# Where the last twelve weighted sums of an attention block stand in TensorE's order

## The chip, the cores and the metric

The kernel runs on one core of a Trainium2 chip. The metric is the device time of one execution in microseconds (us), as the median of several runs. A core has five engines that work through their own queues in order: TensorE (PE; its weight loads are listed as PEld), VectorE (DVE), ScalarE (ACT), GpSimd (POOL) and SyncE (SP, which issues DMAs). They wait for each other by semaphores.

## What is computed

A layer of convolutions and a selective scan, then an additive attention, then a normalised recurrence, on a tensor of 4 images with 128 channels and 4096 positions. The change is in the attention, which for each image computes

```python
q = einsum('bld,ud->blu', x, Wt)            # U = 32 units
k = einsum('bld,ud->blu', x, Wx)
beta = tanh(q[:, :, None, :] + k[:, None, :, :] + bh)
alpha = einsum('bsju,u->bsj', beta, Wa[:, 0]) + ba[0]
alpha = softmax(tanh(alpha), axis=-1)
c_r = einsum('bsj,bjd->bsd', alpha, x)      # the weighted sums
t = t + c_r
```

## The kernel before

`_bounded` runs three stages one after the other: `_layer0` (up to about 3900 us), `_rational` (the attention, to about 11430 us) and `_chunked` (the recurrence). Within each the order of the instructions is written out by hand: an engine runs what the code issues to it in the order in which the code issues it.

`_rational` works through 4 images of 8 blocks each; a block is 512 queries (`QB`), and its tiles are the 32 groups (`JT`) of 128 keys. It doesn't compute the 32 hyperbolic tangents of a pair one by one. It groups the 32 units in six groups, of 6, 6, 5, 5, 5 and 5 units. For each group the sum of the tangents is a fraction, whose denominator and numerator are each one matrix product of exponentials of the keys (`F`) with exponentials of the queries (`E`, and `cE`, weighted). The groups stand in pairs: `A` holds the two groups of six units, each a product over 64 rows; `B1` and `B2` hold two groups of five units each, products over 32 rows. `products` (line 1209) issues them, through `lower` for the denominators and `upper` for the numerators.

For a tile and a pair of groups the work is this:
- `lower` (line 1217): two matmuls on TensorE into one denominator buffer `pd` (two banks of PSUM; the pool has two such buffers).
- `inverse` (line 1229): on ScalarE a logarithm (line 1231), which reads `pd` and so frees it, and an exponential (line 1232). The result is `ra` for `A`, `rb` for `B1` and `B2`.
- `upper` (line 1222): two matmuls into two numerator buffers `pn` (one bank each; the pool has three).
- `times` (line 1225): on VectorE, two multiplications of `ra` or `rb` by the two `pn` (line 1227); each frees one `pn`.
- GpSimd adds the three pairs (lines 1346 and 1333), and VectorE adds the two halves of the sum into `A[:, jt, :]` (line 1343).

Every matmul here is recorded as two instructions (passes). The loop over the tiles is at lines 1323 to 1350. For tile `jt` TensorE gets, in this order: the denominators `dA`; the numerators `nB2` of the tile before; the denominators `dB1`; the numerators `nA`; the denominators `dB2`; the numerators `nB1`. At the end of a tile the list `between` may add work: functions registered for a tile number, called in line 1349.

After the last tile of a block, `A` is turned into weights in four parts (`PARTS`, line 1380) by a tanh and an exponential on ScalarE. The weighted sum of a tile is one matmul over all 128 rows into the buffer `ct` (`weighted`, line 1356, recorded as line 1357), accumulated over the 32 tiles. The sums of tiles 0 to 19 (`NOW` = 20) are issued there. Those of tiles 20 to 31 are left: `between[2 + i]` receives one each, for tiles 2 to 13 of the next block. The division and the output of the old block follow as further entries of `between` in tiles 14 to 22 (`CLOSE_AT`), and the normalisation of the next image, its queries and its transposes also stand in `between`, at tiles 15 to 29. The very last block issues all its sums at once. So 31 of the 32 blocks have twelve such sums in their tiles, 372 in all.

Of the kernel before, what the change touches and what calls it, by code (L numbers as in the profile page):

```python
# [1045 lines left out]
def _rational(ctx, tc, k, x1, x2, top, Wt, Wx, bh, Wa, ba):  # L1046
# [20 lines left out]
    def ln_exp():  # L1067
        nc.scalar.preload_act_table_set("natural_log_exp_and_others")
# [7 lines left out]
    def pw():  # L1076
        return psW.tile([P, QB], F32, name="ct", tag="ct")
# [62 lines left out]
    def norm_load(b, xn, cols):  # L1140
        nc.sync.dma_start(xn[:, cols], x1[b, :, cols])

    def norm_steps(xn, cols, alloc):

        xc = xn[:, cols]
        n = cols.stop - cols.start
        held = {}

        def centre():
            ps = alloc()  # L1150
            _mm(nc, ps, k.avg, xc, n)
            nc.vector.tensor_tensor(xc, xc, ps, ALU.subtract)

        def square():
            held["sq"] = rb.tile([P, CH], F32, name="sq", tag="rb")[:, 0:n]
            nc.scalar.activation(held["sq"], xc, AF.Square)

        def rate():
            ps = alloc()
            _mm(nc, ps, k.avg, held["sq"], n)  # L1160
            _rsqrt(nc, held["sq"], ps, k.eps5)

        def scale():
            nc.gpsimd.tensor_tensor(xc, xc, held["sq"], ALU.mult)

        return centre, square, rate, scale

    def keys(F, xn, c, ps, i):

        exponent(ps, w_k, xn[:, blocks[c]], i, F[:, i, blocks[c]], b_k[:, i : i + 1])  # L1170
# [23 lines left out]
    def queries(E, xn, s, i):  # L1194
        exponent(pw(), w_q, xn[:, s * QB : (s + 1) * QB], i, E[:, i, :])
# [21 lines left out]
    def lower(unit, F, jt, E):  # L1217
        ps = pd()
        products((ps[:, 0, :], ps[:, 1, :]), unit, F, jt, E)
        return ps  # L1220

    def upper(unit, F, jt, cE):
        return products((pn(), pn()), unit, F, jt, cE)

    def times(r, ns):
        for a in range(2):
            nc.vector.tensor_tensor(r[:, a, :], r[:, a, :], ns[a], ALU.mult)  # L1227

    def inverse(d, pool, tag):
        r = pool.tile([P, 2, QB], F32, name=tag, tag=tag)  # L1230
        nc.scalar.activation(r, d, AF.Ln, scale=LOWER)  # L1231
        nc.scalar.activation(r, r, AF.Exp, scale=-1.0)  # L1232
        return r
# [58 lines left out]
    start = 0  # L1292
    first = lower("A", F, 0, E), lower("B1", F, 0, E)
    between = {}
    for c in range(1, nq):
        for i in range(2):
            between.setdefault(2 * c - 2 + i, []).append(lambda c=c, i=i, xn=xn: keys(F, xn, c, pw(), i))
    for c in range(nq):
        between.setdefault(16 + c, []).append(lambda c=c, xn=xn: turn(xT, xn, c))
    for b in range(B):  # L1300
        upcoming = None
        for s in range(nq):
            more = s + 1 < nq or b + 1 < B
            turned = s + 1 == nq and b + 1 < B
            xr = sb.tile([P, QB], F32, name="xr")
            nc.sync.dma_start(xr, x1[b, :, blocks[s]])
            if b + 1 < B:

                if s == 0:
                    upcoming = two.tile([P, L], F32, name="xn")  # L1310
                norm_load(b + 1, upcoming, blocks[s])
                for at, go in zip(NORM_AT, norm_steps(upcoming, blocks[s], pn)):
                    between.setdefault(at, []).append(go)
            if more:
                E_next = two.tile([P, 2, QB], F32, name="E")
                of = upcoming if turned else xn
                for i in range(2):
                    between.setdefault(QUERIES_AT[i], []).append(
                        lambda i=i, s=s, of=of, E_next=E_next: queries(E_next, of, (s + 1) % nq, i)
                    )  # L1320
            ln_exp()
            late = None
            for jt in range(start, JT + 1):
                if jt < JT:
                    dA = lower("A", F, jt, E) if jt > start else first[0]
                if late is not None:
                    pj, rA_, rB2_ = late
                    nB2 = upper("B2", F, pj, cE)
                if jt < JT:
                    dB1 = lower("B1", F, jt, E) if jt > start else first[1]  # L1330
                if late is not None:
                    times(rB2_, nB2)
                    nc.gpsimd.tensor_tensor(rA_, rA_, rB2_, ALU.add)  # L1333
                if jt < JT:
                    nA = upper("A", F, jt, cE)
                    rA = inverse(dA, ra, "ra")
                    times(rA, nA)
                    dB2 = lower("B2", F, jt, E)
                    nB1 = upper("B1", F, jt, cE)
                    rB1 = inverse(dB1, rb, "rb")  # L1340
                    times(rB1, nB1)
                if late is not None:
                    nc.vector.tensor_tensor(A[:, pj, :], rA_[:, 0, :], rA_[:, 1, :], ALU.add)  # L1343
                if jt == JT:
                    break
                nc.gpsimd.tensor_tensor(rA, rA, rB1, ALU.add)  # L1346
                rB2 = inverse(dB2, rb, "rb")
                late = jt, rA, rB2
                for go in between.pop(jt, ()):
                    go()  # L1350

            if more:
                E, cE = E_next, weigh(E_next)
            ct = pw()

            def weighted(jt, ct=ct, xT=xT):
                nc.tensor.matmul(ct, xT[:, jt, :], A[:, jt, :], start=(jt == 0), stop=(jt == JT - 1))  # L1357

            held = {}

            def ahead(step):
                if not more:
                    return
                if step == 0:
                    held["A"], held["B1"] = lower("A", F, 0, E), lower("B1", F, 0, E)
                    held["A"] = direct(held["A"], upper("A", F, 0, cE), ra, "ra")
                elif step == 1:
                    held["B2"] = lower("B2", F, 0, E)  # L1370
                    held["B1"] = direct(held["B1"], upper("B1", F, 0, cE), rb, "rb")
                    nc.gpsimd.tensor_tensor(held["A"], held["A"], held["B1"], ALU.add)
                elif step == 2:
                    held["first"] = lower("A", F, 1, E)
                    r = direct(held["B2"], upper("B2", F, 0, cE), rb, "rb")
                    nc.gpsimd.tensor_tensor(held["A"], held["A"], r, ALU.add)
                else:
                    held["first"] = held["first"], lower("B1", F, 1, E)

            for i, (lo, hi) in enumerate(PARTS if more else LAST_PARTS):  # L1380
                nc.scalar.activation(A[:, lo:hi, :], A[:, lo:hi, :], AF.Tanh, bias=b_a)  # L1381
                nc.scalar.activation(A[:, lo:hi, :], A[:, lo:hi, :], AF.Exp)  # L1382
                if i == 0:
                    if turned:

                        F = big.tile([P, 2, L], F32, name="F")
                        for c in range(nq):
                            all_keys(F, upcoming, c)
                    ahead(0)
                if hi <= NOW or not more:  # L1390
                    for jt in range(lo, hi):
                        weighted(jt)
                if more and i + 1 < len(PARTS):
                    ahead(i + 1)
            if more:
                nc.vector.tensor_tensor(A[:, 0, :], held["A"][:, 0, :], held["A"][:, 1, :], ALU.add)
                first = held["first"]
                start = 1
            between = {}

            todo = closing(b, s, ct, xr, 4 if more else 1)
            if more:
                for i, jt in enumerate(range(NOW, JT)):
                    between[2 + i] = [lambda jt=jt, weighted=weighted: weighted(jt)]
                for at, go in zip(CLOSE_AT, todo):
                    between[at] = [go]
            else:
                for go in todo:
                    go()
            if turned:  # L1410
                xn = upcoming
                xT = big.tile([P, JT, P], F32, name="xT")
                for c in range(nq):
                    between.setdefault(22 + c, []).append(lambda xT=xT, xn=xn, c=c: turn(xT, xn, c))
# [247 lines left out]
```

## Time and profile before

| what | value |
|---|---|
| median of 3 runs | 11655.28 us (11652.04 to 11657.58) |
| the profiled execution, its own time | 11654.41 us |
| its span in the profile | 11652.7 us |
| TensorE, VectorE, ScalarE, GpSimd busy, 5000 to 6000 us | 964.60, 744.27, 958.39, 702.72 us |
| L1212, numerators, 12288 instructions | 4728.8 us busy, 650 ns each |
| L1212, denominators, 12288 instructions | 3478.0 us busy, 648 ns each |
| L1231 and L1232 for `rb`, 1986 each | 1011 and 1057 ns each |
| L1227 for `rb`, 3972 instructions | 682 ns each |
| L1346 and L1333 on GpSimd, 993 each | 2653 and 2363 ns each |
| L1357, the weighted sums, 2048 instructions | 641 ns each |

The times of the profile are from one execution, counted from the start of its span. "Busy" is the time in which an engine had an instruction in work; records of TensorE overlap, since products over few rows run side by side in the array, and several are merged into one line of a timeline ("x4"). In a timeline a line has the start, the duration, the engine, the line of code, the operation, what is written and what is read, and in brackets how long the engine stood idle before and what released it. In the list of waits a line has who waited, for whom, the total in us, how many times and the longest.

### The profile page before, as it was taken

To read this page: it belongs to the slowest core of one execution; us is meant where nothing else is said; L and a number is where in the kernel's file an instruction comes from. 1 tells how busy PE (TensorE), PEld (TensorE's weight loads), DVE (VectorE), ACT (ScalarE), POOL (GpSimd) and SP (SyncE) were. 2 spreads that over 40 slices of the span, in tenths; PEclk is the share of its full clock that TensorE was granted. 3 is DMA by queue.
4 is the path that set the end of the run, shared out by engine and by line. 5 is a ranking of instruction groups with operands and counts; after the bars stand their busy time and mean duration, and the time that the engine had idled before them with its cause. 6 is when DMAs were issued, how large, how long until landed. Compare 5 with 4: busy or idle time off the path is not lost.

```text
span 11652.7 us, 111820 instructions
## 1 busy us (share of the span) xinstructions
PE 10307.6 (88%) x36210; PEld 3184.3 (27%) x36210; DVE 8997.6 (77%) x10066; ACT 9520.9 (82%) x10209; POOL 8625.1 (74%) x3703
## 2 busy tenths in 40 slices
PE   6787787778777699999999999999999999999997
PEld 2121121122111133333333333333333333333334
DVE  4998899889889677777777777777777777777773
ACT  3566556656655599999999999999999999999996
POOL 3999889889889677767766776767677767776773
PEclk8898898889888799999999999999999999999998
DMA  4888778778778300000000000000000000000001
GB/s 118 189 182 194 171 177 193 170 182 190 179 171 186 79 1 3 6 3 3 6 3 3 3 6 3 3 3 6 3 3 3 6 2 3 3 4 3 2 3 60
DMA packets 225332, 737.77 MB, mean 63 GB/s; under 512 B 41104, under 2 KB 41936, under 8 KB 223712
## 3 DMA queue, kind: packets, MB, share of 16 engines
q1 hardware_dynamic: 221760, 729.96, 26.5%
q8 instruction: 286, 4.69, 0.2%
q14 instruction: 310, 2.54, 0.1%
q10 hardware_dynamic: 2976, 0.58, 0.0%
HBM read 612.95 MB, written 117.44 MB: 63 GB/s over the span
## 4 chain that ended last, share of the span: by engine, by line
PE 50%; ACT 9%; DVE 4%; issue 3%; POOL 0%; DMA 0%; DVEq 0%; POOLq 0%; SPq 0%; ACTq 0%
PE pn L1212 26%; PE pd L1212 16%; PE ct L1357 4%; ACT A L1381 3%; ACT A L1382 2%; DVE rb L1227 2%; ACT rb L1231 1%; ACT rb L1232 1%; PE ct L1134 1%; ACT ra L1231 1%; DVE rb L1239 1%; PE vy L1556 0%; DVE A L1343 0%; PE pn L56 0%; PE ct L1262 0%
## 5 line engine op out<-in xcount | busy, mean ns | idle before, releaser
L1212 PE MATMUL pn<-cE,F 32*128 32x512 f32 (+1 forms) x12288 | 4728.8, 650 | 196.6 <-DVE rb L1227 88.5
L1227 DVE TENSOR_TENSOR rb<-rb,pn 128x512 f32<-128x512 f32 x3972 | 2544.5, 682 | 1310.9 <-PE pd L1212 684.9
L1212 PE MATMUL pd<-E,F 32*128 32x512 f32 (+1 forms) x12288 | 3478.0, 648 | 20.9 <-DVE ra L1239 15.7
L1346 POOL TENSOR_TENSOR ra<-ra,rb 128x1024 f32<-128x1024 f32 x993 | 2634.5, 2653 | 957.2 <-DVE rb L1227 956.9
L1333 POOL TENSOR_TENSOR ra<-ra,rb 128x1024 f32<-128x1024 f32 x993 | 2346.8, 2363 | 409.0 <-DVE rb L1227 348.4
L626 POOL TENSOR_TENSOR dBu<-dtdu,bbcc 128x1024 f32<-128x1024 f32 x1024 | 2398.3, 2368 | 216.9 <-DMA dtdu<-ddd 155.5
L1232 ACT ACTIVATE rb<-rb 128x1024 f32<-128x1024 f32 x1986 | 2099.6, 1057 | 62.8
L1212 PEld LDWEIGHTS pn<-cE,F 32*128 32x128 f32 (+1 forms) x12288 | 1418.0, 185 | 2574.8 <-DVE rb L1227 1066.6
L1231 ACT ACTIVATE rb<-pd 128x1024 f32<-128x1024 f32 x1986 | 2007.6, 1011 | 89.9 <-PE pn L1212 75.2
L668 PE MATMUL py<-h,gather 128*32 128x512 f32 x4096 | 1297.9, 699 | 477.3 <-POOL h L651 364.5
L1227 DVE TENSOR_TENSOR ra<-ra,pn 128x512 f32<-128x512 f32 x1986 | 1317.9, 684 | 231.4 <-ACT ra L1232 175.6
L1212 PEld LDWEIGHTS pd<-E,F 32*128 32x128 f32 (+1 forms) x12288 | 931.4, 185 | 1638.5 <-issue 693.7
L621 ACT ACTIVATE pa<-dtdu,a_neg 128x1024 f32<-128x1024 f32 x1024 | 1145.3, 1119 | 53.1 <-DVE h L641 32.1
L651 POOL TENSOR_TENSOR h<-h,bbcc 128x1024 f32<-128x1024 f32 x384 | 912.0, 2375 | 346.2 <-ACT carry L649 338.5
L641 DVE TENSOR_TENSOR_SCAN pa<-pa,carry,dBu 128x1024 f32<-128x1024 f32 x480 | 1124.7, 2343 | 23.1 <-ACT pa L621 11.3
L1232 ACT ACTIVATE ra<-ra 128x1024 f32<-128x1024 f32 x993 | 1049.6, 1057 | 31.4
L1357 PE MATMUL ct<-A,xT 128*128 128x512 f32 x2048 | 1050.9, 641 | 8.2 <-ACT A L1382 8.2
L1231 ACT ACTIVATE ra<-pd 128x1024 f32<-128x1024 f32 x993 | 1008.7, 1016 | 60.0 <-PE pd L1212 26.5
L649 ACT COPY carry<-pa 128x1 f32<-128x1 f32 x640 | 102.4, 160 | 1043.7 <-DVE h L648 1041.9
L1343 DVE TENSOR_TENSOR A<-ra 128x512 f32<-128x512 f32 x993 | 745.0, 750 | 116.3 <-POOL ra L1333 116.0
L648 DVE TENSOR_TENSOR h<-pa,bbcc 128x1024 f32<-128x1024 f32 x640 | 784.1, 1225 | 59.0 <-PE py L668 0.9
L641 DVE TENSOR_TENSOR_SCAN h<-pa,carry,dBu 128x1024 f32<-128x1024 f32 x288 | 675.0, 2344 | 171.1 <-PE py L668 148.2
(291 smaller groups left out, 8731.3 us busy)
## 6 DMA issues: line engine op xcount, KB each, us to landing
bbcc<-bcd SPq DMA_DIRECT2D x1024, 256.0 KB, 6.9
dtdu<-ddd SPq DMA_DIRECT2D x1024, 256.0 KB, 7.1
ddd<-dd SPq DMA_DIRECT2D x64, 1024.0 KB, 5.1
src<-src SPq DMA_DIRECT2D x64, 512.0 KB, 8.3
xs<-in_x_dram SPq DMA_DIRECT2D x16, 512.0 KB, 7.5
src<-xs SPq DMA_DIRECT2D x16, 512.0 KB, 3.0
bcd<-bc SPq DMA_DIRECT2D x64, 128.0 KB, 2.0
src<-xsT SPq DMA_DIRECT2D x16, 512.0 KB, 5.4
```

The source lines that it names most:

```text
L621: nc.scalar.activation(dA, its[m].DT[r][:, 0, :], AF.Exp, scale=a)
L626: nc.gpsimd.tensor_tensor(dBu, its[m].DT[r][:, 1, :], its[m].BC[q][:, 0, :], ALU.mult)
L641: nc.vector.tensor_tensor_scan(to[:, step], dA[:, step], live.pop(("dBu", u))[:, step], 0.0 if m % nch == 0 else its[m - 1].carry[:, col : ...
L651: nc.gpsimd.tensor_tensor(h, h, cc, ALU.mult)
L668: nc.tensor.matmul(it.y[to, c], gather, live["h", v][:, c], start=False, stop=(q == QS - 1))
L1212: nc.tensor.matmul(ps[a], F[lo:hi, i, jt * P : (jt + 1) * P], side[lo:hi, i, :], start=True, stop=True)
L1227: nc.vector.tensor_tensor(r[:, a, :], r[:, a, :], ns[a], ALU.mult)
L1231: nc.scalar.activation(r, d, AF.Ln, scale=LOWER)
L1232: nc.scalar.activation(r, r, AF.Exp, scale=-1.0)
L1333: nc.gpsimd.tensor_tensor(rA_, rA_, rB2_, ALU.add)
L1346: nc.gpsimd.tensor_tensor(rA, rA, rB1, ALU.add)
L1357: nc.tensor.matmul(ct, xT[:, jt, :], A[:, jt, :], start=(jt == 0), stop=(jt == JT - 1))
```

## The change

The twelve sums are registered in a second list, `middle`, which is called at another place of the tile: after `dB1` and after the multiplication and addition of `B2` of the tile before, and ahead of `nA`. The tile numbers stay 2 to 13. All other entries of `between` stay where they are.

```diff
--- before
+++ after
@@ -1292,6 +1292,7 @@
     start = 0
     first = lower("A", F, 0, E), lower("B1", F, 0, E)
     between = {}
+    middle = {}
     for c in range(1, nq):
         for i in range(2):
             between.setdefault(2 * c - 2 + i, []).append(lambda c=c, i=i, xn=xn: keys(F, xn, c, pw(), i))
@@ -1331,6 +1332,8 @@
                 if late is not None:
                     times(rB2_, nB2)
                     nc.gpsimd.tensor_tensor(rA_, rA_, rB2_, ALU.add)
+                for go in middle.pop(jt, ()):
+                    go()
                 if jt < JT:
                     nA = upper("A", F, jt, cE)
                     rA = inverse(dA, ra, "ra")
@@ -1401,7 +1404,7 @@
             todo = closing(b, s, ct, xr, 4 if more else 1)
             if more:
                 for i, jt in enumerate(range(NOW, JT)):
-                    between[2 + i] = [lambda jt=jt, weighted=weighted: weighted(jt)]
+                    middle[2 + i] = [lambda jt=jt, weighted=weighted: weighted(jt)]
                 for at, go in zip(CLOSE_AT, todo):
                     between[at] = [go]
             else:
```

TensorE's order in tiles 2 to 13 was `dA`, `nB2`, `dB1`, `nA`, `dB2`, `nB1`, sum; it becomes `dA`, `nB2`, `dB1`, sum, `nA`, `dB2`, `nB1`.

## The prediction

> **What bounds the kernel now.** I read the page's busy times and its chain first, then the waits inside the attention stretch (4200 to 11200 us), then the timeline of single tiles.
>
> ```profile
> PE 10307.6 (88%) x36210; PEld 3184.3 (27%) x36210; DVE 8997.6 (77%) x10066; ACT 9520.9 (82%) x10209; POOL 8625.1 (74%) x3703
> ...
> PE pn L1212 26%; PE pd L1212 16%; PE ct L1357 4%; ACT A L1381 3%; ACT A L1382 2%; DVE rb L1227 2%; ACT rb L1231 1%; ACT rb L1232 1%; PE ct L1134 1%; ACT ra L1231 1%; DVE rb L1239 1%; PE vy L1556 0%; DVE A L1343 0%; PE pn L56 0%; PE ct L1262 0%
> ```
>
> The chain names TensorE, and in the attention TensorE is busy 0.97 of the time, but ScalarE is at 0.96 beside it (windows of 1000 us), so a busy share decides nothing. The waits say what TensorE lacks:
>
> ```profile
> PEld pn L1212 <- DVE rb L1227: 1013.0, 1381, 2.9
> DVE rb L1227 <- PE pd L1212: 660.8, 688, 2.5
> PEld pn L1212 <- DVE ra L1227: 210.8, 346, 1.5
> ```
>
> The numerators (`pn`) wait for a PSUM bank that VectorE's multiplication L1227 gives back. Now one tile that holds a weighted sum (I call it the sum matmul; L1357, two passes):
>
> ```profile
> 6208.88 1.13 PE L1212 MATMUL pd<-E,F 64*128 64x512 f32 x4
> 6209.94 0.70 PE L1212 MATMUL pn<-cE,F 32*128 32x512 f32 x2
> 6210.06 1.02 ACT L1231 ACTIVATE ra<-pd 128x1024 f32<-128x1024 f32 x1
> 6211.01 2.02 PE L1212 MATMUL pn<-cE,F 64*128 64x512 f32 x4
> 6211.17 1.28 DVE L1227 TENSOR_TENSOR rb<-rb,pn 128x512 f32<-128x512 f32 x2 [1.36 <-PE pd L1212]
> 6211.91 0.29 PEld L1212 LDWEIGHTS pn<-cE,F 64*128 64x128 f32 x2 [0.61 <-DVE rb L1227]
> 6212.37 1.39 DVE L1227 TENSOR_TENSOR ra<-ra,pn 128x512 f32<-128x512 f32 x2
> 6212.97 0.70 PE L1212 MATMUL pd<-E,F 32*128 32x512 f32 x2
> 6214.16 1.12 PE L1357 MATMUL ct<-A,xT 128*128 128x512 f32 x2
> 6214.20 1.02 ACT L1231 ACTIVATE rb<-pd 128x1024 f32<-128x1024 f32 x1
> 6215.21 0.70 PE L1212 MATMUL pd<-E,F 64*128 64x512 f32 x2
> ```
>
> and one that holds none and no other extra work:
>
> ```profile
> 6320.28 0.70 PE L1212 MATMUL pn<-cE,F 32*128 32x512 f32 x2
> 6321.30 1.01 ACT L1231 ACTIVATE ra<-pd 128x1024 f32<-128x1024 f32 x1
> 6323.43 1.29 DVE L1227 TENSOR_TENSOR ra<-ra,pn 128x512 f32<-128x512 f32 x2 [0.63 <-ACT ra L1232]
> 6324.17 0.29 PEld L1212 LDWEIGHTS pn<-cE,F 32*128 32x128 f32 x2 [0.56 <-DVE ra L1227]
> 6325.22 1.13 PE L1212 MATMUL pd<-E,F 64*128 64x512 f32 x4
> 6326.28 0.70 PE L1212 MATMUL pn<-cE,F 32*128 32x512 f32 x2
> ```
>
> The second tile is bound by ScalarE: three Ln/Exp pairs at 2.00 us each, 6.00 us from one start of the logarithm `ra<-pd` to the next. The first is bound by TensorE: 6.33 us (6208.88 to 6215.21). There six-unit numerators `A` (6211.01) take 2.02 us, where the same form for the denominators takes 1.13: their second half stands still until 6211.91 for the bank of `rb`. The timeline gives the same cadence for all 31 blocks that hold such sums: tile 2 takes 6.15, tiles 3 to 13 6.33 each (a handful of stray tiles apart, by about 0.2), tile 14 6.16. Their sum is 6.15 + 11 x 6.33 + 6.16 = 81.94 us; ScalarE alone would need 13 x 6.00 = 78.00.
>
> **What the Trainium skill says.** "Perfetto Trace Analysis", Identifying the Most-Contended Engine, warns that matmul busy time is no measure of nearness to peak; the trace agrees, as the 2.02 us record holds 0.9 us of waiting. The same page, Identifying Performance Opportunities, reads a gap that repeats as a want of buffers; here it is the third `pn` bank. "TensorEngine Tiling (Array Packing)", Key Properties, says that a change of tiling mode drains TensorE. The sum matmul (full array) stands between a 32-row and a 64-row group before and after, so a tile has five changes either way; the trace shows 1.05 us from the sum matmul to the next group (6214.16 to 6215.21), no visible drain. "TensorE: Matmul & The Clock Gate", What's actually happening, puts the array at half rate after idle windows of 3.4 us that run freely; the clock record here has half-rate stretches of 3.4, 6.8 and 10.2 us. I use that below.
>
> **The change, part by part.** Per tile 2 to 13 of 31 blocks, one sum matmul (372 in all) goes from the end of TensorE's tile to the place between `dB1` and `nA`. Nothing is added or removed; no DMA and no instruction of another queue moves, and VectorE's and GpSimd's orders stay. On TensorE it is moved past `nA`, `dB2` and `nB1`. Its data (a slice of `A` of the old block, `xT`) were ready before the block began, so it waits for nothing.
>
> I set zero at the start of the group `nB2`+`dB1` (6209.94) and carry the lags of the two tiles over.
> - The group: 1.07 (6209.94 to 6211.01). The sum matmul: 1.05, so it ends at 2.12.
> - VectorE starts on `rB2` at 1.23 and returns its first bank 0.74 later (6211.17 to 6211.91), at 1.97. So `nA` finds both banks at 2.12: the stall of 0.90 is filled, by a matmul of 1.05.
> - What is late next: `nB1`'s second half needs the bank of `nA`'s first half, that is `times(rA)`. In today's sum tile `nA`'s first half runs ahead alone, and `rA` starts at 2.43, so `nB1` loses only 0.13 (the group from 6212.97 takes 1.19). Now `nA` starts at 2.12, `rA` at 2.12 + 1.23 = 3.35, its bank returns at 4.09 (0.74, also 6323.43 to 6324.17), `nB1` ends 1.05 later (6324.17 to 6325.22) at 5.14, `dA` of the next tile takes 1.06, and the next group starts at 6.20.
>
> The tile without a sum checks this sum: there `rA` starts at 3.15, because the exponential ends then, and 3.15 + 0.74 + 1.05 + 1.06 = 6.00. So the new sum tile takes 6.20 on TensorE against 6.33, and ScalarE's 6.00 is not reached. The move trades 0.90 of stall at `nA` for one of 0.77 more at `nB1`.
>
> Over a block: on entry TensorE is 1.02 us ahead of the logarithm (6320.28 against 6321.30; tile 2 the same) and loses 0.20 per tile. Tiles 2 to 5 therefore keep ScalarE's 6.00 (24.00). Then `dB2`, which ends at 2.12 + 1.05 + 1.23 = 4.40, holds the third logarithm: tile 6 takes 6.18, tiles 7 to 13 6.20 each (43.40), tile 14 6.06 as the lead comes back. Sum 79.64, against 81.94: 2.30 us per block, times 31 = 71 us. Covers: VectorE has 0.84 us to spare before `rA` at 3.35 (free at 2.51), the exponential ends near 2.30, GpSimd needs 2.36 + 2.67 = 5.03 per tile. None is short.
>
> Against this stands the half-rate clock. Once a block, in tile 22, VectorE holds TensorE up for 2.08 us or more, and by its phase against the 3.41 us grid that tile takes 7.78 (no half rate, blocks 10, 12, 14), about 9.3 (one window), or about 10.8 (two). The mean of blocks 1 to 23 is 9.54, 1.76 over 7.78. Blocks 3 to 6 and 18 to 22 sit at a period near 228.8, which is 67 windows (228.7), with one window each. A shorter block leaves this lock: its bare period goes from 227.16 to 224.86, 0.42 under 66 windows, so the phase walks through all cases. Following the phase by the prices above I get mostly two windows in two blocks of three: (2 x 3.05 + 1.55)/3 = 2.5 a block, up 0.7. Over 23 blocks that is 17 us given back; I take 14, since each turn to a new image sets the phase anew. Bounds from both sides: no half rate at all in these tiles gives 1.76 x 23 = 40 us more gain, two windows in each (3.05 - 1.76) x 23 = 30 us less.
>
> Sum against the profiled execution: span 11652.7, execution 11654.41; minus 71, plus 14 gives 11597.4. The median of the runs shown, 11655.28, is 0.9 above, so 11598 us.
>
> **The rivals.**
> - Full gain: `nB1` doesn't stall, and the sum tiles fall to ScalarE's 6.00. 3.94 x 31 = 122 us, 11533. For it: TensorE's work is only 5 x 1.06 = 5.3 us per tile. Against: the wait for `ra` at 6324.17 is there already in the tile without a sum.
> - No gain: `times(rB2)` is made to wait for the sum matmul too, or the half-rate windows take it. With the first, `rB2` starts at 2.28, its bank returns at 3.02, `nA`'s second half ends at 4.08, and 1.19 + 1.06 lead to 6.33: no difference, 11655. For it: today's wait names the `pd` matmul right ahead in the queue. Against: the multiplications are issued ahead of the sum matmul, so they have no reason to wait for it. The clock alone takes at most 30 of 71.
> - Slower: the full-array sum matmul between two groups that feed VectorE drains the array, where it costs nothing visible today, and `nA`'s results, `rA` and the bank for `nB1` all come late. From 0.18 us per tile (period 6.38) it outweighs the gain; at 0.30 the tiles take 6.50, the thirteen 12 x 6.50 - 0.82 (the lead) + 6.06 = 83.2, 1.3 x 31 = 40 us more: 11695. For it: `nA` lies on the chain and today's place has slack behind it. Against: the 1.05 us above, with the same neighbours.
>
> **How the numbers follow.** Partial gain 0.63 (its own range 11560 to 11632), full gain 0.09 (11500 to 11560), no gain 0.15 (11632 to 11678), slower 0.13. The range 11530 to 11675 leaves out the slower case and half of the full gain, under 2 in 10. A change of 0.2%, 23 us, is about what a measurement can tell from none. Faster: 0.63 + 0.09, less 0.02 of the first near its edge, 0.70. Within: 0.16. Slower: 0.14.
>
> **What would show it.** Right: logarithm starts 6.00 apart in tiles 2 to 5 and 6.20 in 7 to 13; the row of `pn` weight loads waiting for `rb` falls by some 0.61 x 372 = 227 us and that for `ra` grows by about 0.56 x 372 = 208 us (the recorded gaps at 6211.91 and 6324.17); `nA` in 1.13 us. Wrong: 6.33 or more in tiles 7 to 13 (no gain, slower), 6.00 in all (full), or tile 22 above 10.5 in every block.

## The result, and the profile after

The changed kernel takes 11598.17 us (median of 5 runs, 11595.65 to 11604.05), the kernel before in runs beside it 11653.49. The ratio is 0.9953, with a 95% interval of 0.9942 to 0.9964: faster by 0.5%, 55 us. The profiled execution took 11599.52 us, its span 11597.8, which is 54.9 less than the span before.

The page of the changed kernel, busy times and chain, looks almost as it did:

```profile
PE 10265.4 (89%) x36210; PEld 3139.3 (27%) x36210; DVE 8992.9 (78%) x10066; ACT 9467.7 (82%) x10209; POOL 8626.5 (74%) x3703
...
PE pn L1212 26%; PE pd L1212 16%; PE ct L1360 4%; ACT A L1384 4%; ACT A L1385 2%; DVE rb L1227 2%; ACT rb L1231 1%; ACT rb L1232 1%; PE ct L1134 1%; ACT ra L1231 1%; PE vy L1559 1%; DVE A L1346 0%; PE ct L1262 0%; PE pn L56 0%; ACT L1384 0%
```

Shares don't tell the two apart; the change is seen in a tile. The added lines shift the line numbers: the sum is now L1360, GpSimd's additions are L1334 and L1349, VectorE's is L1346. This is a tile with a sum in the timeline of the changed kernel:

```profile
6179.27 0.70 PE L1212 MATMUL pn<-cE,F 32*128 32x512 f32 x2
6180.34 1.12 PE L1360 MATMUL ct<-A,xT 128*128 128x512 f32 x2
6180.50 1.28 DVE L1227 TENSOR_TENSOR rb<-rb,pn 128x512 f32<-128x512 f32 x2 [0.89 <-ACT ra L1231]
6181.40 0.30 PEld L1212 LDWEIGHTS pn<-cE,F 64*128 64x128 f32 x4 [0.76 <-DVE rb L1227]
6181.40 1.13 PE L1212 MATMUL pn<-cE,F 64*128 64x512 f32 x4
6182.46 0.70 PE L1212 MATMUL pd<-E,F 32*128 32x512 f32 x2
6182.62 1.29 DVE L1227 TENSOR_TENSOR ra<-ra,pn 128x512 f32<-128x512 f32 x2 [0.84 <-PE pn L1212]
```

The sum runs while VectorE frees `rb`'s bank; `nA` (6181.40) then needs 1.13 us where it took 2.02. One tile earlier in the same timeline the other end is seen: the multiplication `ra` waits for `nA`, and `nB1`'s second half for that.

```profile
6173.06 0.70 PE L1212 MATMUL pn<-cE,F 32*128 32x512 f32 x2
...
6176.42 1.28 DVE L1227 TENSOR_TENSOR ra<-ra,pn 128x512 f32<-128x512 f32 x2 [0.84 <-PE pn L1212]
6176.79 1.49 PE L1212 MATMUL pn<-cE,F 32*128 32x512 f32 x3
6177.16 0.29 PEld L1212 LDWEIGHTS pn<-cE,F 32*128 32x128 f32 x2 [0.61 <-DVE ra L1227]
6178.21 1.13 PE L1212 MATMUL pd<-E,F 64*128 64x512 f32 x4
```

From one group `nB2`+`dB1` to the next it is 6.21 us (6173.06 to 6179.27), against 6.33. The waits between 4200 and 11200 us, one line of the kernel before and then three of the changed one:

```profile
DVE ra L1227 <- PE pn L1212: 24.1, 41, 1.0
```

```profile
PEld pn L1212 <- DVE rb L1227: 1333.6, 1728, 2.9
...
PEld pn L1212 <- DVE ra L1227: 416.6, 686, 1.4
...
DVE ra L1227 <- PE pn L1212: 320.3, 387, 1.2
```

The last was 24.1 us before: VectorE now waits 0.84 us in most sum tiles. The one for `ra` grew by 206. The one for `rb` rose, although the wait it is named for is gone. The timeline shows why: the load at 6181.40 carries "0.76 <-DVE rb", but by the 0.74 us that a bank took to return before, it was free near 6181.24 (6180.50 + 0.74), and the load starts only 1.06 after the sum's start. I read this as the load standing behind the running sum: the name is that of the semaphore that came last, not of what held the engine.

From the starts of the logarithm `ra<-pd` in both traces, the span's 54.9 us divide like this (a tile's time is from its own logarithm to the next tile's):

| stretch | before | after | difference |
|---|---|---|---|
| tiles 2 to 14 of blocks 1 to 31 | 2541.8 (81.99 a block) | 2477.3 (79.91 a block) | -64.4 |
| tile 22 of blocks 1 to 23 | 219.4 (9.54 each) | 231.1 (10.05 each) | +11.7 |
| the other tiles from 15 to 30 | 2956.0 | 2951.4 | -4.6 |
| everything else | | | +2.4 |

Of the -4.6, 3.4 us lie in tiles 24 and 25 of blocks 24 to 31. There is no next image to normalise there, and in six of these blocks TensorE stands still for 1.8 us in tile 24, not in tile 22.

### The profile page after: what moved, and what is told of

It reads as the page before. It is cut to its first block, busy times and chain, and to the rows that moved or that the text cites. A ratio compares the mean times of both kernels' runs of the same rounds, so it can differ in the third digit from the quotient of the medians.

```text
span 11597.8 us, 111820 instructions
## 1 busy us (share of the span) xinstructions
PE 10265.4 (89%) x36210; PEld 3139.3 (27%) x36210; DVE 8992.9 (78%) x10066; ACT 9467.7 (82%) x10209; POOL 8626.5 (74%) x3703
## 3 DMA queue, kind: packets, MB, share of 16 engines
q14 instruction: 311, 2.54, 0.1%
## 4 chain that ended last, share of the span: by engine, by line
PE 50%; ACT 10%; DVE 3%; issue 3%; POOL 0%; DMA 0%; POOLq 0%; DVEq 0%; SPq 0%; ACTq 0%
PE pn L1212 26%; PE pd L1212 16%; PE ct L1360 4%; ACT A L1384 4%; ACT A L1385 2%; DVE rb L1227 2%; ACT rb L1231 1%; ACT rb L1232 1%; PE ct L1134 1%; ACT ra L1231 1%; PE vy L1559 1%; DVE A L1346 0%; PE ct L1262 0%; PE pn L56 0%; ACT L1384 0%
## 5 line engine op out<-in xcount | busy, mean ns | idle before, releaser
L1349 POOL TENSOR_TENSOR ra<-ra,rb 128x1024 f32<-128x1024 f32 x993 | 2637.0, 2656 | 1077.5 <-DVE rb L1227 1077.3
L1334 POOL TENSOR_TENSOR ra<-ra,rb 128x1024 f32<-128x1024 f32 x993 | 2345.6, 2362 | 228.4 <-DVE rb L1227 123.9
L1232 ACT ACTIVATE rb<-rb 128x1024 f32<-128x1024 f32 x1986 | 2099.5, 1057 | 62.9
L1212 PEld LDWEIGHTS pn<-cE,F 32*128 32x128 f32 (+1 forms) x12288 | 1367.1, 186 | 2553.9 <-DVE rb L1227 1386.2
L1227 DVE TENSOR_TENSOR ra<-ra,pn 128x512 f32<-128x512 f32 x1986 | 1288.2, 683 | 528.1 <-PE pn L1212 325.0
L1232 ACT ACTIVATE ra<-ra 128x1024 f32<-128x1024 f32 x993 | 1049.7, 1057 | 31.4
L1360 PE MATMUL ct<-A,xT 128*128 128x512 f32 x2048 | 1052.3, 642 | 8.8 <-ACT A L1385 8.8
L1346 DVE TENSOR_TENSOR A<-ra 128x512 f32<-128x512 f32 x993 | 743.3, 749 | 115.9 <-POOL ra L1334 115.8
```

Source lines behind the costliest of these rows:

```text
L1212: nc.tensor.matmul(ps[a], F[lo:hi, i, jt * P : (jt + 1) * P], side[lo:hi, i, :], start=True, stop=True)
```

## The experiments

The kernel before took 11653.28 to 11655.79 us beside them.

**The sum right behind `dA`.** If only a matmul that runs while `nA` waits is free, this place must give nothing.

```diff
                     dA = lower("A", F, jt, E) if jt > start else first[0]
+                for go in middle.pop(jt, ()):
+                    go()
...
-                for go in middle.pop(jt, ()):
-                    go()
```

> The sums of tiles 2 to 13 stand right behind dA, ahead of nB2 and dB1; the rest is as in the changed kernel. My theory (only a matmul that runs while nA's second half waits for rB2's bank is free): nA stalls 0.9 us again, the sum adds its 1.05 us to TensorE's chain, tiles 3 to 13 take 6.33 us, the whole 11645 to 11665 us. Rival (what mattered was to take the sum away from the place ahead of dA, so that the next logarithm isn't held): dA is now ahead of the sum, so tiles should take 6.0 to 6.2 us, the whole 11540 to 11600 us.

Measured: 11652.76 us, ratio 0.9999 (0.9990 to 1.0008). Its timeline:

```profile
6178.35 1.12 PE L1360 MATMUL ct<-A,xT 128*128 128x512 f32 x2
6179.40 0.70 PE L1212 MATMUL pn<-cE,F 32*128 32x512 f32 x2
...
6180.47 2.02 PE L1212 MATMUL pn<-cE,F 64*128 64x512 f32 x4
...
6184.68 1.12 PE L1360 MATMUL ct<-A,xT 128*128 128x512 f32 x2
```

6.33 us from sum to sum and 2.02 for `nA`, as expected: the stall is back, and so is the time. To take the sum off the place ahead of `dA` is worth nothing by itself; the rival falls.

**The sum behind `nA`.** Ahead of `dB2` and `nB1` instead.

```diff
-                for go in middle.pop(jt, ()):
-                    go()
...
                     times(rA, nA)
+                    for go in middle.pop(jt, ()):
+                        go()
                     dB2 = lower("B2", F, jt, E)
```

> The sums of tiles 2 to 13 stand behind nA, ahead of dB2 and nB1. My theory: nA's second half stalls as before; the sum covers the wait of nB1 for rA's bank, but it puts dB2 off until 4.08 us after the group nB2+dB1, its logarithm starts at 5.31 and frees the denominators' buffer for the next dB1 at 6.35: tiles of 6.35 us, the whole 11650 to 11670 us. Rival (any place within the tile in which a numerator waits is as good as the other): 6.2 us, 11590 to 11605 us.

Measured: 11623.41 us, ratio 0.9974 (0.9964 to 0.9985), between the two expectations. Its timeline:

```profile
6176.11 0.70 PE L1212 MATMUL pn<-cE,F 32*128 32x512 f32 x2
6176.29 0.70 PE L1212 MATMUL pd<-E,F 32*128 32x512 f32 x2
6177.35 1.87 PE L1212 MATMUL pn<-cE,F 64*128 64x512 f32 x4
6179.15 1.12 PE L1360 MATMUL ct<-A,xT 128*128 128x512 f32 x2
6180.21 0.70 PE L1212 MATMUL pd<-E,F 32*128 32x512 f32 x2
6182.34 0.70 PE L1212 MATMUL pn<-cE,F 32*128 32x512 f32 x2
```

The tile takes 6.23, not the 6.35 that I had worked out. I had the denominators' buffer hold the whole group `nB2`+`dB1`. The trace shows the two apart by 0.18: `nB2` goes ahead of `dB1`, in other rows of the array, and it alone feeds the chain through `rb`, on which the second half of `nA` waits. So a sum tile takes nearly the same whichever of the two stalls is filled, and the other one stays (1.87 for `nA` here). What is lost is the beginning: `dB2` is late from tile 2 on (6.31 in the median, then 6.23), so the block has no tiles at 6.00, and tiles 2 to 14 take 80.88 us against 79.91: 30 us more over 31 blocks, where the medians differ by 25.

**The sum in two halves.** Both stalls filled, each with half of the columns (`HALF` is `QB // 2`, and `second` a list like `middle`).

```diff
...
-            def weighted(jt, ct=ct, xT=xT):
-                nc.tensor.matmul(ct, xT[:, jt, :], A[:, jt, :], start=(jt == 0), stop=(jt == JT - 1))
+            def weighted(jt, ct=ct, xT=xT, lo=0, hi=QB):
+                nc.tensor.matmul(
+                    ct[:, lo:hi], xT[:, jt, :], A[:, jt, lo:hi], start=(jt == 0), stop=(jt == JT - 1 and hi == QB)
+                )
...
                     times(rA, nA)
+                    for go in second.pop(jt, ()):
+                        go()
                     dB2 = lower("B2", F, jt, E)
...
-                    middle[2 + i] = [lambda jt=jt, weighted=weighted: weighted(jt)]
+                    middle[2 + i] = [lambda jt=jt, weighted=weighted: weighted(jt, hi=HALF)]
+                    second[2 + i] = [lambda jt=jt, weighted=weighted: weighted(jt, lo=HALF)]
```

> Each sum of tiles 2 to 13 is cut into two matmuls of 256 columns: one ahead of nA (the place of the change), one behind nA, ahead of dB2 and nB1. My theory: the first half (0.53 us) lets nA's first half go at 1.60, rA starts at 2.83 and frees its bank at 3.57, when the second half ends (3.56); neither numerator stalls much, TensorE's chain is 5.7 us, so ScalarE's 6.00 us bounds all of tiles 2 to 14: 1.9 us per block less than the changed kernel, 59 us in all, 11540 us, with some 25 us either way from the half-rate windows. Rival (twice as many weight loads and short passes cost what the stall gives back): 6.2 us per tile or more, 11595 us or above.

Measured: 11526.34 us, ratio 0.9892 (0.9875 to 0.9908), 14 us below the 11540 expected and within its 25. Its timeline (the logarithm is L1232 here, the products L1213):

```profile
6146.73 1.00 ACT L1232 ACTIVATE ra<-pd 128x1024 f32<-128x1024 f32 x1
6146.85 0.70 PE L1364 MATMUL ct<-A,xT 128*128 128x256 f32 x2
6147.48 1.32 PE L1213 MATMUL pn<-cE,F 64*128 64x512 f32 x4
6148.73 0.70 PE L1364 MATMUL ct<-A,xT 128*128 128x256 f32 x2
6149.36 0.70 PE L1213 MATMUL pd<-E,F 32*128 32x512 f32 x2
6152.74 1.01 ACT L1232 ACTIVATE ra<-pd 128x1024 f32<-128x1024 f32 x1
```

6.01 us from one logarithm to the next; tiles 2 to 14 take 78.09 us a block. A half costs 0.63 us (6146.85 to 6147.48), not half of 1.05: cutting in two costs 0.2 us of TensorE per tile, and it doesn't matter here, since ScalarE binds.

**One half ahead of `nA`, the other at the end of the tile.** As above, but `second` is called next to `between`.

> Each sum is cut into two matmuls of 256 columns: one ahead of nA, one at the end of the tile, where the sums stood before the change. My theory: nA[0] at 1.60, rA at 2.83, its bank at 3.57, nB1's second half until 4.62, the second half of the sum until 5.15, dA until 6.21: 6.2 us per tile as in the changed kernel, 11585 to 11615 us. Rival (the gain is in proportion to the stall of nA that is filled, 0.53 of 0.90): 6.26 us and more, 11620 us or above.

Measured: 11674.60 us, ratio 1.0017 (1.0011 to 1.0024), slower than before. It is outside my range. It lies in the rival's, which was open upwards, but a gain in proportion to the filled stall can't turn into a loss. Its timeline:

```profile
6187.72 1.02 ACT L1232 ACTIVATE ra<-pd 128x1024 f32<-128x1024 f32 x1 [0.16 <-PE pd L1213]
6188.67 0.70 PE L1364 MATMUL ct<-A,xT 128*128 128x256 f32 x2
6192.33 0.70 PE L1364 MATMUL ct<-A,xT 128*128 128x256 f32 x2
6194.13 1.02 ACT L1232 ACTIVATE ra<-pd 128x1024 f32<-128x1024 f32 x1 [0.16 <-PE pd L1213]
```

Its tiles take 6.41. The two halves cost 0.10 more each than I had assumed (0.63 for 0.53), and both lie on TensorE's chain: 6.21 + 0.20 = 6.41. The order of the waits was right, the price was not.

**Sums left out.** Does the work of the sums still count when both stalls hold it? This kernel leaves out the twelve sums of each block, so its result is not that of the attention (the accumulation ends with tile 19 in a part of the edit that is not shown).

```diff
...
-                for i, jt in enumerate(range(NOW, JT)):
-                    middle[2 + i] = [lambda jt=jt, weighted=weighted: weighted(jt)]
```

> The sums of key tiles 20 to 31 are left out of blocks 0 to 30 (the weighted sums then cover 20 of 32 tiles). My theory: the twelve sums in halves already cost nothing in time, so this gives the same as them: tiles 2 to 13 at 6.00 us, ScalarE's rate, 11510 to 11545 us. Rival (TensorE's work in these tiles still counts): 372 x 1.05 us of matmul less, a time clearly below 11500 us.

Measured: 11522.46 us, ratio 0.9887 (0.9870 to 0.9903), and 78.00 us for tiles 2 to 14. Two of its logarithms in a row:

```profile
6142.91 1.00 ACT L1231 ACTIVATE ra<-pd 128x1024 f32<-128x1024 f32 x1
...
6148.91 1.00 ACT L1231 ACTIVATE ra<-pd 128x1024 f32<-128x1024 f32 x1
```

Without any sum the tiles are no faster than ScalarE's 6.00; the sums in halves are hidden but for some 4 us, no more than the executions of one kernel differ by.

**Tile 22.** The half-rate windows (stretches of 3.4 us, or two of them, in which the clock record grants TensorE half its clock) were the prediction's second term. TensorE's stall there begins on GpSimd. The timeline of the changed kernel:

```profile
6250.98 1.27 POOL L1164 TENSOR_TENSOR xn<-xn,sq 128x512 f32<-128x512 f32 x1
6252.22 2.35 POOL L1334 TENSOR_TENSOR ra<-ra,rb 128x1024 f32<-128x1024 f32 x1
6254.53 2.35 POOL L1349 TENSOR_TENSOR ra<-ra,rb 128x1024 f32<-128x1024 f32 x1
6254.60 2.84 DVE L1346 TENSOR_TENSOR A<-ra 128x512 f32<-128x512 f32 x1 [0.41 <-POOL ra L1334]
6258.09 2.07 PE L1212 MATMUL pn<-cE,F 64*128 64x512 f32 x2 [2.07 <-DVE rb L1227]
...
6263.52 0.68 DVE L1346 TENSOR_TENSOR A<-ra 128x512 f32<-128x512 f32 x1
6263.75 2.67 POOL L1349 TENSOR_TENSOR ra<-ra,rb 128x1024 f32<-128x1024 f32 x1 [2.60 <-DVE rb L1227]
```

The step of 1.27 us puts GpSimd's addition off, VectorE waits 0.41 for it, starts its own addition (0.69 else) 0.07 after GpSimd's next, and takes 2.84. "SBUF — State Buffer", Who interferes with whom, has this: an instruction of VectorE with two SBUF inputs and one of GpSimd that reads SBUF exclude each other, and whoever comes second stands still. The trace agrees: VectorE's addition ends 0.56 after GpSimd's (6257.44 and 6256.88), and in the changed kernel all 30 additions of VectorE that begin while GpSimd's runs take 2.81 to 2.86, the other 994 about 0.7. The last two lines are the other order: GpSimd's addition begins 0.23 after VectorE's and takes 2.67 instead of 2.35. TensorE then stands idle for 2.07, and from 6258.09 on its matmuls take about twice their time; the clock record has half rate from 6257.39 on, for 6.83 us.

First only this step was cut into two halves, for tiles 20 and 21:

```diff
-        def scale():
-            nc.gpsimd.tensor_tensor(xc, xc, held["sq"], ALU.mult)
+        def scale(lo=0, hi=n):
+            nc.gpsimd.tensor_tensor(xc[:, lo:hi], xc[:, lo:hi], held["sq"][:, lo:hi], ALU.mult)
```

> The changed kernel with GpSimd's last step of the normalisation (1.27 us, registered for tile 20) cut into two halves for tiles 20 and 21. My theory of tile 22: this step makes GpSimd late, VectorE's add then runs into GpSimd's next add and takes 2.83 us, TensorE stands still for 2 us and more and the half-rate windows come from that. GpSimd has 6.00 - 5.03 us to spare per tile, so 0.64 us fits: tile 22 falls from 10.0 us to 6.2 to 7.0 in blocks 1 to 23, without a half-rate window there: 70 us less, 11520 to 11540 us. Rival (the windows come by themselves at that distance from the last ones and cost their 1.5 to 3 us in any tile): 7.8 to 10 us remain in tile 22 or beside it, 11570 us or above.

Measured: 11573.20 us, ratio 0.9930 (0.9914 to 0.9947): 25 us of the 70, and the time that the rival gave. Tile 22 fell to 6.19 in the mean, but tile 24 rose from 6.48 to 9.15 in the median, with the half-rate windows now there. So by this run alone the windows could indeed come by themselves. But its timeline shows a second stall, of the same kind, with another step, the closing addition to `xr`:

```profile
6253.09 1.27 POOL L1264 TENSOR_TENSOR xr<-xr,rec 128x512 f32<-128x512 f32 x1
6254.33 2.36 POOL L1336 TENSOR_TENSOR ra<-ra,rb 128x1024 f32<-128x1024 f32 x1
6256.67 2.36 POOL L1351 TENSOR_TENSOR ra<-ra,rb 128x1024 f32<-128x1024 f32 x1
6256.72 2.85 DVE L1348 TENSOR_TENSOR A<-ra 128x512 f32<-128x512 f32 x1 [0.20 <-POOL ra L1336]
6260.23 1.75 PE L1212 MATMUL pn<-cE,F 64*128 64x512 f32 x2 [1.78 <-DVE rb L1227]
```

With the sums in halves as well:

> Sums in halves and the normalisation's last step in two, together. My theory: both gains add up, as they lie in different tiles: 11526 less some 70 us, 11440 to 11475 us. Rival (the second gain belongs to the phase of the half-rate windows, not to the stall): 11500 us or above.

Measured: 11497.93 us, ratio 0.9864 (0.9847 to 0.9880), 28 us below the halves alone, with the stall in tile 24 here too (9.09). It is just outside the rival's range and further from mine; what sets the two theories apart is to cut the second step as well.

**Both steps in two**, the closing addition too (half in tile 22, half in 23), in three kernels. Of the edit only the part on the closing addition is shown:

```diff
...
-            nc.gpsimd.tensor_tensor(xr, xr, held["rec"], ALU.add)
-            nc.sync.dma_start(x2[b, :, blocks[s]], xr)
+            add(0, QB // 2)
+
+        def add(lo, hi):
+            nc.gpsimd.tensor_tensor(xr[:, lo:hi], xr[:, lo:hi], held["rec"][:, lo:hi], ALU.add)
+
+        def rest():
+            add(QB // 2, QB)
+            nc.sync.dma_start(x2[b, :, blocks[s]], xr)
```

> The kernel before the change, with both of GpSimd's extra steps cut into two halves: the normalisation's last step (tiles 20 and 21) and the closing addition to xr (tiles 22 and 23). My theory: VectorE's add no longer runs into GpSimd's late add in tile 22 or 24, TensorE doesn't stand still there, so no half-rate windows between 100 and 170 us of a block; tiles 22 and 24 near 6.2 and 6.5 us: 11540 to 11575 us. Rival (half-rate windows fall there anyway): above 11600 us.

> The changed kernel with the same two cuts. My theory: freed of the half-rate windows, the change is worth what the tiles 2 to 14 show, 82.0 - 79.9 = 2.1 us in each of 31 blocks: 65 us less than the kernel before with the two cuts (60 to 70), 11475 to 11510 us. Rival (the windows aren't what took the rest): 55 us again or less.

> Sums in halves, with the same two cuts. My theory: another 1.8 us per block, 57 us less than the changed kernel with the two cuts: 11415 to 11450 us, the fastest of all. Rival (a block without the stalls is held by something else): above 11470 us.

| sums | median, us | ratio to the kernel before | tiles 2 to 14, us a block |
|---|---|---|---|
| as before the change | 11545.54 | 0.9907 (0.9892 to 0.9922) | 81.99 |
| as after it | 11485.39 | 0.9855 (0.9840 to 0.9870) | 79.94 |
| in halves | 11426.50 | 0.9804 (0.9790 to 0.9817) | 78.09 |

All three lie in the ranges expected. In all three the clock record has no half-rate stretch between 100 and 170 us of blocks 1 to 31 (counted from a block's first logarithm `ra<-pd`), where the kernel before has 25 (123 us in sum) and the changed one 26 (143 us). Tile 22 takes 6.19. This is its end in the changed kernel with both cuts, where the additions are L1342, L1354 and L1357:

```profile
6221.99 0.73 POOL L1164 TENSOR_TENSOR xn<-xn,sq 128x256 f32<-128x256 f32 x1
6222.69 2.35 POOL L1342 TENSOR_TENSOR ra<-ra,rb 128x1024 f32<-128x1024 f32 x1
6225.13 0.68 DVE L1354 TENSOR_TENSOR A<-ra 128x512 f32<-128x512 f32 x1
6225.35 2.68 POOL L1357 TENSOR_TENSOR ra<-ra,rb 128x1024 f32<-128x1024 f32 x1 [0.32 <-DVE rb L1227]
```

VectorE's addition comes first again and takes 0.68. The change itself is then worth 60.2 us, at the lower end of the 60 to 70 expected; tiles 2 to 14 give 2.05 x 31 = 63.6, and where the remaining 3 us lie I did not follow up. The last kernel is the fastest of this study.

## Why the prediction was right

- **The stall of `nA` is filled.** `nA` takes 1.13 us, as said. Shown also by the reverse: behind `dA`, where no one waits, the same matmul costs what it cost at the end of the tile.
- **What is late next is `nB1`, by way of `rA`.** The trace has `rA` waiting 0.84 for `nA` and the load of `nB1` for `rA`. The tile takes 6.21; the sum said 6.20.
- **The lead of a block.** I gave four tiles at 6.00; three have it, then 6.11 and 6.21, then 6.05 in tile 14. The lead on entry is as said (1.03 from the group at 6129.53 to the logarithm at 6130.56), but tile 2 takes 0.28 of it, since `dB1` there still waits 0.09 for its buffer (6129.53 and 6129.62). That, with the 0.01 per tile and a few stray tiles, makes 79.91 a block for 79.64: 64 us for 71.
- **The half-rate windows give back.** 14 us taken. Tile 22 costs 11.7 more, and tiles 24 and 25 of blocks 24 to 31 give 3.4 of it back. That the windows follow the stall, and aren't bound to the distance from the last ones, is shown: with both steps cut they are gone there.
- **The phase decides how many.** The clock records of the nine profiles that have the stall agree with the prediction. In each, every half-rate stretch begins on one grid of 3.413 us, to 0.01 us. From the start of a stall to the next step of that grid it is 1.32 to 2.80 us in all 89 stalls with two windows; it is 0 to 0.83 or 2.54 to 3.36 in the 126 with one, and 0.67 to 1.30 in the 40 with none. The ranges overlap only near their edges. In the changed kernel two, two and one window follow each other in blocks 2 to 4, 5 to 7, 9 to 11, 12 to 14 and 20 to 22, the pattern that the prediction had worked out. Of blocks 1 to 23, 13 have two windows, 8 one and 2 none; before it was 7, 12 and 4.
- **Luck in the total.** Two misses, some 7 us too much gain and some 6 too much loss, nearly cancel: the forecast was 57 us less, the profiled executions differ by 55. That it met the median to 1 us is luck. The phases are those of one profile of each kernel.
- **The rivals.** Full gain: what forbids it is the wait that was named, for `nB1`, and filling that too (the halves) brings it. No gain through a wait of `rB2` for the sum: it starts at 6180.50, within the sum. A drain around the sum: the group behind it starts 1.06 after it (6180.34 to 6181.40), for 1.05 before.
- **A wrong sign to watch for.** I had said that the row of `pn` loads waiting for `rb` would fall by 227 us; it rose by 321, for the reason given with that row. The row for `ra` was right (208 said, 206 measured), though as 340 more waits at 0.61 us each and not 372 at 0.56.

## What to carry to other kernels

Work without waits of its own is free only where its engine's queue stands still, and only as far as the next wait of the loop doesn't move along with it: follow the loop until it closes before counting the gain. Where filling one stall only moves it to the next wait, cut the filler in two and put a half at each, as long as another engine is the bound in the end; with one half elsewhere the cut made things worse. And read a small extra step by the slack of its engine per round: 1.27 us on an engine with 0.97 to spare cost over 3 us elsewhere.

## What was not expected of the hardware

- One addition on VectorE took 2.84 us for 0.69 because GpSimd's had started 0.07 earlier, 30 times in the profile of before and 30 in that of the changed kernel; with both extra steps cut the mean of that addition is 685 ns for 750.
- A stall of TensorE of 1.8 to 2.1 us was followed by half-rate windows of 3.4 or 6.8 us in most blocks and by none in a few (blocks 17, 18 and 26 of the changed kernel, blocks 10, 12, 14 and 16 before) with the same stall. That fits the free-running grid of "TensorE: Matmul & The Clock Gate", What's actually happening; but that section has half rate after an idle window of about 3.4 us, and here stalls of 1.78 us were enough. By its phase alone one stall costs 0, 1.5 or 3 us more.
- A matmul over half the columns cost 0.63 us for 1.05 of the whole.
